# A row LSTM behind a group normalisation: first block's loads spread over the statistics, first chunk in four pieces, weights behind the fourth chunk, last block stored in two parts

## The chip, the cores and the metric

The kernel runs on one core of a Trainium2 chip. The metric is the device time in microseconds (us) of one execution. Six executions of the kernel before lie between 2173.32 and 2176.66 us. Engine names: PE is TensorE (matmul), PEld its weight loads, DVE is VectorE, ACT is ScalarE, POOL is GpSimd, SP is SyncE, which issues most DMAs.

## The reference, cut to what matters

```python
# x: (8, 96, 128, 128) float32
x = x + conv_lstm(group_norm(x))        # 32 groups of 3 channels, over whole images

def conv_lstm(X):                        # rows of the image are the time steps
    its = conv(X, W_is * mask)           # input-to-state, 384 outputs
    for row in range(128):
        gates = conv(h, W_ss) + its[row]
        f, i, o, g = ...                 # three sigmoids, one tanh
        c = f * c + i * g
        h = o * tanh(c)                  # h is the output row
```

The statistics need all of x (50.33 MB) before the first row can be normalised. Then 128 rows follow one another. Images are treated in two halves (s = 0, 1) of four, so there are 256 half steps, and the rows come in blocks of four (R = 4).

## The kernel before

Three parts matter: what the queues load before the recurrence, in which order VectorE works there, and the last store.

```python
# weights, issued from ScalarE at the start
nc.scalar.dma_start(wt[0:C, 0, :], w_ss[:, 0])
# ... six more weight loads, two of the bias, one of the group matrix, from ScalarE
nc.vector.tensor_add(wr[:, 0, :], wt[:, 0, :], wt[:, 3, :])
# ... three more sums on VectorE, one of the bias

def load_rows(s, k):           # 64 channels, once into each half of the partitions
    nc.sync.dma_start(xr[s][0:C2, :, 1:], rows_of(s, k, 0, C2))
    nc.sync.dma_start(xr[s][C2:P, :, 0 : R * W], rows_of(s, k, 0, C2))

def load(s, k):                # 32 channels into partitions 96-127, 96 into 0-95
    t = x_pool.tile([P, BH, R, W], F32, tag=f"x{s}", name=f"x{s}_{k}")
    flat = t.rearrange("c b r w -> c b (r w)")
    nc.sync.dma_start(flat[C:P], rows_of(s, k, C2, C))
    nc.sync.dma_start(flat[0:C], rows_of(s, k, 0, C))
    xt[s, k] = t

# statistics: 48 chunks of 128 x 8 KB through a ring of four tiles
for b in range(B):
    # ...
    for k in range(QW // CH):
        xc = ring[n % len(ring)]
        n += 1
        nc.sync.dma_start(xc, xb[:, bass.ts(k, CH)])
        for j in range(CH // SN):
            nc.vector.bn_stats(bst[:, k * (CH // SN) + j, :], xc[:, bass.ts(j, SN)])
        if n == len(ring):
            for s in range(NH):          # the first block, behind the fourth chunk
                load_rows(s, 0)
                load(s, 0)
    nc.vector.bn_aggr(st[:, b, :], bst.rearrange("c n s -> c (n s)"))

# products that nobody reads: 112 over 128, 64 and 32 rows; ten more just before the recurrence
# ...
# at the end of each row (in HalfStep.output): the residual
nc.gpsimd.tensor_add(xo, xo, h)
# at the end of each block of four rows:
def store(s, k):
    nc.sync.dma_start(out[... 4 rows ...], xt.pop((s, k))[0:C]...)
```

Call a load **wide** if it fills all 128 partitions (the chunks), and **narrow** if it fills 32, 64 or 96 of them (the eight DMAs of the first block, 4.19 MB together, in rows of 2 KB).

Of the kernel before, what the change touches and what calls it, by code (L numbers as in the profile page):

```python
# [7 lines left out]
F32 = mybir.dt.float32  # L8
# [7 lines left out]
def strided(ap, offset, dims):  # L16

    return bass.AP(ap.tensor, ap.offset + offset, [ap.ap[0], *[list(d) for d in dims]])
# [3 lines left out]
def kernel(  # L22
# [28 lines left out]
    nc = tc.nc  # L51
    B, C, H, W = x.shape
    P = 128
    NH = 2
    BH = B // NH
    R = 4
    NB = H // R
    J = W // 2
    JP = J + 2
    C2 = 64  # L60
    HW = H * W
    QW = C * HW // P
    CH = R * BH * W
# [3 lines left out]
    const = ctx.enter_context(tc.tile_pool(name="const", bufs=1))  # L67
    x_pool = ctx.enter_context(tc.tile_pool(name="xblk", bufs=2))
    g_pool = ctx.enter_context(tc.tile_pool(name="gates", bufs=2))
    ps_pool = ctx.enter_context(  # L70
        tc.tile_pool(name="ps", bufs=2, space=bass.MemoryType.PSUM)
    )
    ps_st = ctx.enter_context(
        tc.tile_pool(name="ps_st", bufs=1, space=bass.MemoryType.PSUM)
    )




    wt = const.tile([P, 5, 4 * C], F32, name="wt")  # L80
    wr = const.tile([P, 2, 4 * C], F32, name="wr")
    nc.scalar.dma_start(wt[0:C, 0, :], w_ss[:, 0])
    nc.scalar.dma_start(wt[C:P, 0, :], w_is[C2:C, 0])
    nc.scalar.dma_start(wr[0:C, 1, :], w_ss[:, 1])
    nc.scalar.dma_start(wr[C:P, 1, :], w_is[C2:C, 1])
    nc.scalar.dma_start(wt[0:C, 3, :], w_ss[:, 2])
    nc.gpsimd.memset(wt[C:P, 3, :], 0.0)
    nc.scalar.dma_start(wt[0:C2, 4, :], w_is[0:C2, 0])
    nc.scalar.dma_start(wt[C2:P, 4, :], w_is[0:C2, 1])

    for a in range(3):
        for j in range(4):
            third = a if j == 3 else j
            cols = bass.ds(a * P + j * 32, 32)
            if third < 2:
                nc.gpsimd.memset(wr[C:P, 1, cols], 0.0)
            if third < 1:
                nc.gpsimd.memset(wt[C:P, 4, cols], 0.0)
    nc.vector.tensor_add(wr[:, 0, :], wt[:, 0, :], wt[:, 3, :])
    nc.vector.tensor_add(wt[:, 1, :], wr[:, 0, :], wr[:, 1, :])  # L100
    nc.vector.tensor_sub(wt[:, 2, :], wr[:, 0, :], wr[:, 1, :])
    nc.vector.tensor_scalar_mul(wt[:, 1:3, :], wt[:, 1:3, :], 0.5)

    bias = const.tile([P, 3], F32, name="bias")
    bias2 = const.tile([P, 3], F32, name="bias2")
    nc.scalar.dma_start(bias, b_ss)
    nc.scalar.dma_start(bias2, b_is)
    nc.vector.tensor_add(bias, bias, bias2)
    gm = const.tile([P, 3, P], F32, name="gm")
    nc.scalar.dma_start(gm, gmat)  # L110


    def pair(shape, name):
# [20 lines left out]
    xt = {}  # L134

    def rows_of(s, k, lo, hi):
        return x[s * BH : (s + 1) * BH, lo:hi, k * R : (k + 1) * R, :].rearrange(
            "b c r w -> c b (r w)"
        )

    def load_rows(s, k):
        nc.sync.dma_start(xr[s][0:C2, :, 1:], rows_of(s, k, 0, C2))
        nc.sync.dma_start(xr[s][C2:P, :, 0 : R * W], rows_of(s, k, 0, C2))

    def load(s, k):
# [5 lines that stand above are left out]
# [5 lines left out]
    ] + [xn[s][1].rearrange("p r t b j -> p (r t b j)") for s in range(NH)]  # L156
    st = const.tile([P, B, 2], F32, name="st")
    n = 0
    for b in range(B):
        bst = g_pool.tile([P, QW // SN, 6], F32, tag="bst", name=f"bst{b}")  # L160
        xb = x[b].rearrange("c h w -> (c h w)").rearrange("(p q) -> p q", p=P)
        for k in range(QW // CH):
            xc = ring[n % len(ring)]
            n += 1
            nc.sync.dma_start(xc, xb[:, bass.ts(k, CH)])
            for j in range(CH // SN):
                nc.vector.bn_stats(bst[:, k * (CH // SN) + j, :], xc[:, bass.ts(j, SN)])
            if n == len(ring):
                for s in range(NH):
                    load_rows(s, 0)  # L170
                    load(s, 0)
        nc.vector.bn_aggr(st[:, b, :], bst.rearrange("c n s -> c (n s)"))



    def spin(rows, count):
        banks = [
            ps_pool.tile([P, 512], F32, tag=f"ps{a}", name=f"spin{a}_{rows}_{i}")
            for i in range(2)
            for a in range(2)  # L180
        ]
        for i in range(count):
            for q in range(P // rows):
                at = bass.ds(q * rows, rows)
                nc.tensor.matmul(  # L185
                    banks[(q * rows // 32 + i % (rows // 32)) % 4][:, 0:256],
                    wt[at, 0, 0:P],
                    wt[at, 0, 0:256],
                    start=True,
                    stop=True,  # L190
                    skip_group_check=True,
                )


    mean = const.tile([P, 3, B], F32, name="mean")
# [46 lines left out]
    NT = NB * R  # L242
# [4 lines left out]
    def inputs(s, row):  # L247

        h = hx[s][row // R % 2][:, row % R]
        vs, vf = gt("vs", s, row, (P, HB)), gt("vf", s, row, (P, HB))  # L250
        vd = gt("vd", s, row, (P, 2, HB))
        shaped = "p (b j) -> p b j"
        e, o = h[:, 0, :, 0:J], h[:, 1, :, 1 : J + 1]
        nc.vector.tensor_add(vs.rearrange(shaped, b=BH), e, o)  # L254
        last = nc.vector.tensor_sub(vf.rearrange(shaped, b=BH), o, e)  # L255
        diff = nc.gpsimd.tensor_sub(  # L256
            vd.rearrange("p t (b j) -> p t b j", b=BH),
            strided(h[:, 0, 0, :], 1, [(BH * JP - 1, 2), (JP, BH), (1, J)]),
            strided(h[:, 0, 0, :], 0, [(BH * JP + 1, 2), (JP, BH), (1, J)]),
        )  # L260
        tc.add_manual_dep(
            diff.ins,
            last.ins.name,
            mybir.DependencyInfo(mybir.DependencyClass.Sync, mybir.DependencyReason.SCHED_ONLY),
            reason="GpSimd starts when VectorE is done with both SBUF reads",
        )
        return vs, vf, vd

    class HalfStep:
# [62 lines left out]
        def output(self):  # L332

            s, row = self.s, self.row
            nxt = hx[s][(row + 1) // R % 2][0:C, (row + 1) % R]
            h = strided(nxt[:, 0, 0, :], 0, [(BH * JP + 1, 2), (JP, BH), (1, J)])
            shaped = "p (t b j) -> p t b j"
            nc.vector.tensor_mul(  # L338
                h,
                self.ps[2][0:C].rearrange(shaped, t=2, b=BH),  # L340
                self.th.rearrange(shaped, t=2, b=BH),
            )
            self.moving = inputs(s, row + 1) if row + 1 < NT else None
            xo = xt[s, row // R][0:C, :, row % R, :].rearrange("p b (j t) -> p t b j", t=2)
            nc.gpsimd.tensor_add(xo, xo, h)  # L345

    def store(s, k):
        nc.sync.dma_start(
            out[s * BH : (s + 1) * BH, :, k * R : (k + 1) * R, :].rearrange(
                "b c r w -> c b (r w)"  # L350
            ),
            xt.pop((s, k))[0:C].rearrange("c b r w -> c b (r w)"),
        )

    OWN, SHARED = ((0, 1), (2,), (), (3,)), ((), (0, 1), (2, 3), ())
# [1 line left out]
    def prepare(s, row):  # L357

        k, r = row // R + 1, row % R
        if k < NB:  # L360
            for j in OWN[r]:
                normalise_own(nc.gpsimd, s, k, j, 0, R)
                border(nc.gpsimd, s, k, j, 0, R)
            for j in SHARED[r]:
                normalise_shared(nc.gpsimd, s, k, j, 0, R)

    def finish(s, row):
        prepare(s, row)
        k = row // R
        if row % R == R - 1:  # L370
            if k + 2 < NB:
                load_rows(s, k + 2)
            store(s, k)
            if k + 2 < NB:
                load(s, k + 2)

    E = mybir.EngineType
    for count in (12, 4):
        for rows in (P, 64, 32):
            spin(rows, count)  # L380
    with tc.manual_schedule(engines={E.PE, E.Activation, E.DVE, E.Pool}):
        pm = ps_st.tile([P, 3, B], F32, tag="pm", name="pm")
        pv = ps_st.tile([P, 2, B], F32, tag="pv", name="pv")
        for i in (2, 0, 1):
# [4 lines left out]
        nc.vector.tensor_add(dq, dq, st[:, :, 1])  # L389
        for i in range(2):  # L390
            nc.tensor.matmul(pv[:, i, :], gm[:, i, :], dq, start=True, stop=True)
        spin(P, 10)
        nc.vector.tensor_scalar(v, pv, 1.0 / GQ, GN_EPS, ALU.mult, ALU.add)
        nc.scalar.activation(t1, v, AF.Sqrt)
        nc.scalar.activation(table, t1[:, 0, 0:1], AF.Sigmoid)
# [30 lines left out]
        for row in range(NT):  # L426
            for s in range(NH):
# [18 lines left out]
                if prev:  # L446
                    prev.cell_tanh()
                    prev.output()
                    moving[prev.s] = prev.moving
                    finish(prev.s, prev.row)  # L450
# [62 lines left out]
```

## Time and profile before

| | kernel before |
|---|---|
| time, median of 6 runs | 2174.74 us (2173.32 to 2176.66) |
| span of the profiled run | 2171.9 us |
| first product of the recurrence | 163.75 us |
| recurrence, first to last product | 1998.0 us |
| last product to the end | 10.1 us |
| VectorE busy, idle up to its last statistic | 121.6 us, and 31.0 us of waits |
| clock of TensorE in the recurrence | 1.00 |

The profile is read in this way. The page's slices give the busy tenths of each engine in 40 equal parts of the span, and below them the granted clock, the busy share of the DMA engines and their rate. The waits name for each engine and line who ended its idle time: us in total, times, longest. The timeline gives start and duration of instructions, with the idle time before the first in square brackets.

### The profile page before, as it was taken

The page shows a single profiled execution, that of the slowest core. Times are in us where ns is not written, and L with a number is a line of the kernel's source. Part 1 is how long each engine was busy: PE and PEld are TensorE (multiplying, and loading weights), DVE is VectorE, ACT ScalarE, POOL GpSimd, SP SyncE. Part 2 cuts the span into 40 slices and gives each one's busy share as a digit, 9 for nine tenths or more (in the row PEclk, how much of TensorE's full clock was granted, in tenths as well). Part 3 has the DMA queues.
Part 4 walks back from the last instruction along what each step waited for, and adds up shares of the span by engine and source line. Part 5 has one row for each costly group of instructions (what it writes and reads, how often), then busy time and mean ns, then how long its engine had stood idle before and what let it go on. Part 6 is the DMA issues. An engine that isn't in the chain of part 4 may idle for free.

```text
span 2171.9 us, 24875 instructions
## 1 busy us (share of the span) xinstructions
PE 2030.3 (93%) x7934; PEld 1465.1 (67%) x7934; DVE 1588.7 (73%) x3299; ACT 1351.5 (62%) x2572; POOL 1028.0 (47%) x1311
## 2 busy tenths in 40 slices
PE   4019999999999999999999999999999999999998
PEld 3017777777777777777777777777777777777775
DVE  4987777777777777777777777777777777777776
ACT  0006666666666666666666666666666666666665
POOL 0006555555555455555544555555455555555542
PEclk8559999999999999999999999999999999999999
DMA  9991444333444443334444332344443334444411
GB/s 304 421 336 39 107 107 107 80 74 74 93 107 107 107 96 78 77 71 106 107 107 107 88 78 76 80 107 107 107 107 81 75 74 92 107 107 107 100 37 29
DMA packets 103297, 237.42 MB, mean 109 GB/s; under 512 B 6304, under 2 KB 6912, under 8 KB 97024
## 3 DMA queue, kind: packets, MB, share of 16 engines
q1 hardware_dynamic: 102144, 234.90, 42.7%
q8 instruction: 64, 1.05, 0.2%
q10 hardware_dynamic: 1024, 0.94, 0.2%
q14 instruction: 65, 0.53, 0.1%
HBM read 185.49 MB, written 50.33 MB: 109 GB/s over the span
## 4 chain that ended last, share of the span: by engine, by line
PE 92%; DVE 0%; issue 0%; POOLq 0%; POOL 0%; ACT 0%
PE ps L283 92%; DVE hx L208 0%; POOLq L508 0%; POOL x L345 0%; DVE ps L300 0%; DVE ps L299 0%; DVE xn L208 0%; DVE hx L338 0%; DVE c L324 0%; ACT m L293 0%; DVE vs L254 0%; DVE nmr L402 0%; DVE rstd L401 0%; DVE nmr L403 0%; DVE t L399 0%
## 5 line engine op out<-in xcount | busy, mean ns | idle before, releaser
L283 PEld LDWEIGHTS ps<-vd,wt 128*128 128x128 f32 x3072 | 583.7, 190 | 407.1 <-issue 366.7
L283 PE MATMUL ps<-xn,wt 128*128 128x512 f32 x1536 | 795.3, 599 | 0.1
L283 PE MATMUL ps<-vd,wt 128*128 128x256 f32 x3072 | 788.4, 379 | 0.0
L256 POOL TENSOR_TENSOR vd<-hx 128x512 f32<-128x512 f32 x256 | 266.5, 1041 | 1080.2 <-DVE vf L255 895.0
L309 ACT ACTIVATE g<-ps 32x512 f32<-32x512 f32 x768 | 454.2, 591 | 468.6 <-PE ps L283 468.6
L293 ACT ACTIVATE m<-ps,bias 128x256 f32<-128x256 f32 x768 | 358.8, 467 | 169.6 <-PE ps L283 169.6
L283 PE MATMUL ps<-vs,wt 128*128 128x256 f32 x1536 | 456.9, 379 | 0.4 <-DVE vs L254 0.4
L283 PE MATMUL ps<-vf,wt 128*128 128x256 f32 x1536 | 456.8, 379 | 0.0
L317 DVE TENSOR_TENSOR ps<-ps,c 96x512 f32<-96x512 f32 x256 | 178.0, 695 | 376.8 <-ACT ps L313 376.8
L313 ACT ACTIVATE ps<-ps 96x512 f32<-96x512 f32 x768 | 442.9, 577 | 16.1
L300 DVE TENSOR_TENSOR ps<-m,ps 128x256 f32<-128x256 f32 x768 | 329.5, 429 | 26.3
L345 POOL TENSOR_TENSOR x<-x,hx 96x512 f32<-96x512 f32 x256 | 331.5, 1295 | 9.5 <-DVE hx L338 9.5
L299 DVE TENSOR_TENSOR ps<-m,ps 128x256 f32<-128x256 f32 x768 | 324.3, 422 | 15.9
L283 PEld LDWEIGHTS ps<-xn,wt 128*128 128x128 f32 x1536 | 270.7, 189 | 73.3 <-DVE ps L300 31.8
L283 PEld LDWEIGHTS ps<-vs,wt 128*128 128x128 f32 x1536 | 291.8, 190 | 40.4 <-PE spin L185 0.8
L283 PEld LDWEIGHTS ps<-vf,wt 128*128 128x128 f32 x1536 | 291.8, 190 | 39.7
L320 DVE TENSOR_TENSOR g<-ps,g 96x512 f32<-96x512 f32 x256 | 175.8, 687 | 107.1 <-ACT g L309 107.1
L208 POOL TENSOR_SCALAR hx<-x,rstd,nmr 32x512 f32<-32x512 f32 (+1 forms) x256 | 207.9, 812 | 25.4
L208 POOL TENSOR_SCALAR xn<-xr,rstd,nmr 128x512 f32<-128x512 f32 (+1 forms) x256 | 208.3, 814 | 0.2
L338 DVE TENSOR_TENSOR hx<-ps,th 96x512 f32<-96x512 f32 x256 | 173.9, 679 | 0.7 <-ACT th L328 0.7
L324 DVE TENSOR_TENSOR c<-ps,g 96x512 f32<-96x512 f32 x256 | 173.9, 679 | 0.0
L328 ACT ACTIVATE th<-c 96x512 f32<-96x512 f32 x256 | 157.9, 617 | 0.9 <-DVE c L324 0.9
(50 smaller groups left out, 443.3 us busy)
## 6 DMA issues: line engine op xcount, KB each, us to landing
xr<-in_x_dram SPq DMA_DIRECT2D x128, 512.0 KB, 9.3
x<-in_x_dram SPq DMA_DIRECT2D x64, 768.0 KB, 9.5
out_dram<-x SPq DMA_DIRECT2D x64, 768.0 KB, 5.4
xs<-in_x_dram SPq DMA_DIRECT2D x24, 1024.0 KB, 7.0
xn<-in_x_dram SPq DMA_DIRECT2D x24, 1024.0 KB, 6.9
x<-in_x_dram SPq DMA_DIRECT2D x64, 256.0 KB, 6.3
wt<-in_w_ss_dram ACTq DMA_DIRECT2D x2, 144.0 KB, 6.9
wt<-in_w_is_dram ACTq DMA_DIRECT2D x2, 96.0 KB, 6.6
```

The lines of the kernel that those rows point to most:

```text
L208: engine.tensor_scalar(dst, src, scale, shift, ALU.mult, ALU.add)
L256: diff = nc.gpsimd.tensor_sub(vd.rearrange("p t (b j) -> p t b j", b=BH), strided(h[:, 0, 0, :], 1, [(BH * JP - 1, 2), (JP, BH), (1, J)]), ...
L283: nc.tensor.matmul(o, wt[:, p, bass.ts(a, P)], rhs, start=start, stop=stop, skip_group_check=True)
L293: nc.scalar.activation(self.m1, self.ps[a][:, 0:HB], AF.Identity, bias=bias[:, a : a + 1])
L299: nc.vector.tensor_add(lo, self.m1, hi)
L300: nc.vector.tensor_sub(hi, self.m1, hi)
L309: nc.scalar.activation(self.g[a * 32 : (a + 1) * 32], self.ps[a][C:P], AF.Tanh)
L313: nc.scalar.activation(gate, gate, AF.Sigmoid)
L317: nc.vector.tensor_mul(f, f, cs[self.s].rearrange("p t b j -> p (t b j)"))
L320: nc.vector.tensor_mul(self.g, self.ps[1][0:C], self.g)
L324: nc.vector.tensor_add(c, self.ps[0][0:C], self.g)
L345: nc.gpsimd.tensor_add(xo, xo, h)
```

## The change

Its intent, as far as the code shows it: VectorE should start with the first quarter of the first chunk and not with the weights; the first block's loads should no longer stop the statistics in one lump; and the end should wait for a smaller store. The diff, cut to its core:

```diff
-    nc.scalar.dma_start(wt[0:C, 0, :], w_ss[:, 0])
+    def load_weights():
+        nc.sync.dma_start(wt[0:C, 0, :], w_ss[:, 0])
 ...                                    (all ten, now on SyncE)
+    def make_weights():                (memsets and VectorE's sums, called after the statistics)
 ...
+    first = [f for s in range(NH) for f in (lambda s=s: load_rows(s, 0), lambda s=s: load(s, 0))]
 ...
-            nc.sync.dma_start(xc, xb[:, bass.ts(k, CH)])
+            for piece in range(4 if n == 1 else 1):
+                size = CH // 4 if n == 1 else CH
+                nc.sync.dma_start(
+                    xc[:, bass.ts(piece, size)], xb[:, bass.ds(k * CH + piece * size, size)]
+                )
 ...
             if n == len(ring):
-                for s in range(NH):
-                    load_rows(s, 0)
-                    load(s, 0)
+                load_weights()
+            if n % 6 == 0 and first:
+                first.pop(0)()
 ...
-    (112 products over 128, 64 and 32 rows)
+    (96 products over 64 rows, chained through empty instructions of ScalarE)
 ...
-            nc.gpsimd.tensor_add(xo, xo, h)
+            (nc.gpsimd if row + 1 < NT else nc.vector).tensor_add(xo, xo, h)
 ...
-            store(s, k)
+            store(s, k, R - 1 if k + 1 == NB else 0, R)
 ...
+        elif k + 1 == NB and row % R == R - 2:
+            store(s, k, 0, R - 1)
```

More of the change, by code (lines that the diff above doesn't have):

```diff
@@ L69 @@
     g_pool = ctx.enter_context(tc.tile_pool(name="gates", bufs=2))
-    ps_pool = ctx.enter_context(
-        tc.tile_pool(name="ps", bufs=2, space=bass.MemoryType.PSUM)
-    )
-    ps_st = ctx.enter_context(
-        tc.tile_pool(name="ps_st", bufs=1, space=bass.MemoryType.PSUM)
-    )
     wt = const.tile([P, 5, 4 * C], F32, name="wt")
     wr = const.tile([P, 2, 4 * C], F32, name="wr")
-    nc.scalar.dma_start(wt[0:C, 0, :], w_ss[:, 0])
-    nc.scalar.dma_start(wt[C:P, 0, :], w_is[C2:C, 0])
@@ L84 @@
-    nc.scalar.dma_start(wr[0:C, 1, :], w_ss[:, 1])
-    nc.scalar.dma_start(wr[C:P, 1, :], w_is[C2:C, 1])
-    nc.scalar.dma_start(wt[0:C, 3, :], w_ss[:, 2])
-    nc.gpsimd.memset(wt[C:P, 3, :], 0.0)
-    nc.scalar.dma_start(wt[0:C2, 4, :], w_is[0:C2, 0])
-    nc.scalar.dma_start(wt[C2:P, 4, :], w_is[0:C2, 1])
-    for a in range(3):
-        for j in range(4):
-            third = a if j == 3 else j
-            cols = bass.ds(a * P + j * 32, 32)
-            if third < 2:
-                nc.gpsimd.memset(wr[C:P, 1, cols], 0.0)
-            if third < 1:
-                nc.gpsimd.memset(wt[C:P, 4, cols], 0.0)
@@ L99 @@
-    nc.vector.tensor_add(wr[:, 0, :], wt[:, 0, :], wt[:, 3, :])
-    nc.vector.tensor_add(wt[:, 1, :], wr[:, 0, :], wr[:, 1, :])
-    nc.vector.tensor_sub(wt[:, 2, :], wr[:, 0, :], wr[:, 1, :])
-    nc.vector.tensor_scalar_mul(wt[:, 1:3, :], wt[:, 1:3, :], 0.5)
     bias = const.tile([P, 3], F32, name="bias")
     bias2 = const.tile([P, 3], F32, name="bias2")
-    nc.scalar.dma_start(bias, b_ss)
-    nc.scalar.dma_start(bias2, b_is)
-    nc.vector.tensor_add(bias, bias, bias2)
     gm = const.tile([P, 3, P], F32, name="gm")
-    nc.scalar.dma_start(gm, gmat)
+    def load_weights():
+        nc.sync.dma_start(wt[0:C, 0, :], w_ss[:, 0])
+        nc.sync.dma_start(wt[C:P, 0, :], w_is[C2:C, 0])
+        nc.sync.dma_start(wr[0:C, 1, :], w_ss[:, 1])
+        nc.sync.dma_start(wr[C:P, 1, :], w_is[C2:C, 1])
+        nc.sync.dma_start(wt[0:C, 3, :], w_ss[:, 2])
+        nc.sync.dma_start(wt[0:C2, 4, :], w_is[0:C2, 0])
+        nc.sync.dma_start(wt[C2:P, 4, :], w_is[0:C2, 1])
+        nc.sync.dma_start(bias, b_ss)
+        nc.sync.dma_start(bias2, b_is)
+        nc.sync.dma_start(gm, gmat)
@@ new lines, in make_weights @@
+    def make_weights():
+        nc.gpsimd.memset(wt[C:P, 3, :], 0.0)
+        for a in range(3):
+            for j in range(4):
+                third = a if j == 3 else j
+                cols = bass.ds(a * P + j * 32, 32)
+                if third < 2:
+                    nc.gpsimd.memset(wr[C:P, 1, cols], 0.0)
+                if third < 1:
+                    nc.gpsimd.memset(wt[C:P, 4, cols], 0.0)
+        nc.vector.tensor_add(wr[:, 0, :], wt[:, 0, :], wt[:, 3, :])
+        nc.vector.tensor_add(wt[:, 1, :], wr[:, 0, :], wr[:, 1, :])
+        nc.vector.tensor_sub(wt[:, 2, :], wr[:, 0, :], wr[:, 1, :])
+        nc.vector.tensor_scalar_mul(wt[:, 1:3, :], wt[:, 1:3, :], 0.5)
+        nc.vector.tensor_add(bias, bias, bias2)
@@ L168 @@
             if n == len(ring):
-                for s in range(NH):
-                    load_rows(s, 0)
-                    load(s, 0)
+                load_weights()
+            if n % 6 == 0 and first:
+                first.pop(0)()
         nc.vector.bn_aggr(st[:, b, :], bst.rearrange("c n s -> c (n s)"))
-    def spin(rows, count):
-        banks = [
-            ps_pool.tile([P, 512], F32, tag=f"ps{a}", name=f"spin{a}_{rows}_{i}")
-            for i in range(2)
-            for a in range(2)
-        ]
-        for i in range(count):
-            for q in range(P // rows):
-                at = bass.ds(q * rows, rows)
-                nc.tensor.matmul(
-                    banks[(q * rows // 32 + i % (rows // 32)) % 4][:, 0:256],
-                    wt[at, 0, 0:P],
-                    wt[at, 0, 0:256],
-                    start=True,
-                    stop=True,
-                    skip_group_check=True,
-                )
+    make_weights()
@@ new lines, with follow @@
+    E = mybir.EngineType
+    ctx.enter_context(tc.manual_schedule(engines={E.PE, E.Activation}))
+    def follow(ins, other):
+        tc.add_manual_dep(
+            ins.ins,
+            other.ins.name,
+            mybir.DependencyInfo(mybir.DependencyClass.Sync, mybir.DependencyReason.DATA),
+            reason="TensorE's row tiles share a bank",
+        )
+    with tc.tile_pool(name="idle", bufs=1, space=bass.MemoryType.PSUM) as idle:
+        banks = [idle.tile([P, 512], F32, tag=f"i{n}", name=f"idle{n}") for n in range(6)]
+        relay = {}
+        for lag in (5, 1, 2, 3):
+            for k in range(12):
+                for q in range(2):
+                    n = (k - lag * q) % 6
+                    at = bass.ds(64 * q, 64)
+                    mm = nc.tensor.matmul(
+                        banks[n][:, 0:256],
+                        wt[at, 0, 0:P],
+                        wt[at, 0, 0:256],
+                        start=q == 0 or k < lag,
+                        stop=True,
+                        skip_group_check=True,
+                    )
+                    if n in relay:
+                        follow(mm, relay.pop(n))
+                    relay[n] = nc.scalar.nop()
+                    follow(relay[n], mm)
@@ new lines, with spin @@
+    ps_pool = ctx.enter_context(
+        tc.tile_pool(name="ps", bufs=2, space=bass.MemoryType.PSUM)
+    )
+    ps_st = ctx.enter_context(
+        tc.tile_pool(name="ps_st", bufs=1, space=bass.MemoryType.PSUM)
+    )
+    def spin(count):
+        bank = ps_pool.tile([P, 512], F32, tag="ps0", name="spin")
+        for i in range(count):
+            nc.tensor.matmul(
+                bank[:, 0:256],
+                wt[:, 0, 0:P],
+                wt[:, 0, 0:256],
+                start=True,
+                stop=True,
+                skip_group_check=True,
+            )
@@ L344, in output, with store @@
             xo = xt[s, row // R][0:C, :, row % R, :].rearrange("p b (j t) -> p t b j", t=2)
-            nc.gpsimd.tensor_add(xo, xo, h)
-    def store(s, k):
+            (nc.gpsimd if row + 1 < NT else nc.vector).tensor_add(xo, xo, h)
+    def store(s, k, lo, hi):
         nc.sync.dma_start(
-            out[s * BH : (s + 1) * BH, :, k * R : (k + 1) * R, :].rearrange(
+            out[s * BH : (s + 1) * BH, :, k * R + lo : k * R + hi, :].rearrange(
                 "b c r w -> c b (r w)"
             ),
-            xt.pop((s, k))[0:C].rearrange("c b r w -> c b (r w)"),
+            xt[s, k][0:C, :, lo:hi, :].rearrange("c b r w -> c b (r w)"),
         )
@@ L372, in finish @@
                 load_rows(s, k + 2)
-            store(s, k)
+            store(s, k, R - 1 if k + 1 == NB else 0, R)
             if k + 2 < NB:
                 load(s, k + 2)
-    E = mybir.EngineType
-    for count in (12, 4):
-        for rows in (P, 64, 32):
-            spin(rows, count)
-    with tc.manual_schedule(engines={E.PE, E.Activation, E.DVE, E.Pool}):
+        elif k + 1 == NB and row % R == R - 2:
+            store(s, k, 0, R - 1)
+    with tc.manual_schedule(engines={E.DVE, E.Pool}):
         pm = ps_st.tile([P, 3, B], F32, tag="pm", name="pm")
@@ L391 @@
             nc.tensor.matmul(pv[:, i, :], gm[:, i, :], dq, start=True, stop=True)
-        spin(P, 10)
+        spin(10)
         nc.vector.tensor_scalar(v, pv, 1.0 / GQ, GN_EPS, ALU.mult, ALU.add)
```

## The prediction

> **What bounds the kernel now.** I read the core's span and clock first, then the page's slices, the chain that ended last, stretches of the trace with the DMA share, the waits, and the timeline of both ends. The page's slices, the clock row and the rate row:
>
> ```profile
> PE   4019999999999999999999999999999999999998
> ...
> DVE  4987777777777777777777777777777777777776
> ...
> PEclk8559999999999999999999999999999999999999
> DMA  9991444333444443334444332344443334444411
> GB/s 304 421 336 39 107 107 107 80 74 74 93 107 107 107 96 78 77 71 106 107 107 107 88 78 76 80 107 107 107 107 81 75 74 92 107 107 107 100 37 29
> ```
>
> A slice is 54 us. Three of them are the group statistics (DMA and DVE full, PE not needed), 37 are the recurrence (PE full at full clock). The chain in order of time says the same in one piece:
>
> ```profile
> 163.75 2.83 PE ps L283 x12
> 166.57 0.07 issue
> 166.64 1988.21 PE ps L283 x7642
> ```
>
> So the run is 163.75 us before the first product, 1998 us of TensorE without a gap, and about 10 us of tail after the last product (2161.8 to 2171.9). The change leaves the 1998 us alone: the same 256 half steps, the same products. It works on the 163.75 and the 10.[...]
>
> What bounds the front is the question. Its waits, VectorE's and then the queue's own:
>
> ```profile
> DVE bst L167 <- DMA xs<-in_x_dram: 18.7, 1, 18.7
> DVE wr L99 <- DMA wt<-in_w_is_dram: 11.2, 1, 11.2
> ...
> SPq L165 <- DVE bst L167: 86.1, 41, 2.8
> ```
>
> VectorE starts at 11.24 us, since the weight sums stand first in its stream and wait for the weights; it eats four chunks, then idles 18.7 us until the fifth chunk. It looks as if 30 us of VectorE idle time were there to be won. The stretches with the DMA share say otherwise (columns: stretch and its length, busy us of PE, PEld, DVE, ACT, POOL with counts, clock, DMA share, GB/s):
>
> ```profile
> 2.00:11.00 9.00, 3.65 (x10) 3.04 (x11) 0.00 (x0) 0.21 (x1) 1.66 (x13) 1.00 0.92 304
> 11.00:18.00 7.00, 7.00 (x52) 5.96 (x52) 6.76 (x14) 1.07 (x1) 0.74 (x12) 1.00 0.95 349
> 18.00:38.00 20.00, 13.12 (x168) 10.99 (x164) 4.78 (x9) 0.00 (x0) 0.00 (x0) 0.91 1.07 222
> 38.00:150.00 112.00, 0.00 (x0) 0.00 (x0) 107.63 (x179) 0.00 (x0) 0.00 (x0) 0.50 1.01 413
> ```
>
> The DMA engines are full in every row. While VectorE idled (18 to 38 us) they carried the first block, 4.19 MB in rows of 2 KB, at only 222 GB/s; before and after they carried chunks at up to 422. From 38 us on VectorE and DMA are level: six chunks take VectorE 24 x 0.593 + 0.8 = 15.0 us (eight statistics take 4.83 us, so they start 0.593 apart), and 6.29 MB at 420 GB/s are also 15.0 us. So **DMA bounds the front**, and VectorE's late start was hidden beneath it.
>
> [...]xr is loaded in two halves, x in 32 and 96 partitions, at 222 GB/s. [...]the trace has 413 to 422 for whole chunks[...]. [...]304 and 349 GB/s in the first two rows, where both issue, are less than the 420 with one. [...]The trace: half until 161.4, 4.3 us after the ten warming products began at 157.07, and full when the recurrence starts at 163.75.
>
> **The change part by part.**
>
> 1. First block spread (one of four 1 MB loads after chunks 6, 12, 18, 24). It removes no byte and widens no load. Each load takes 1.05 MB / 222 GB/s = 4.7 us of all DMA engines, and VectorE, level with DMA, has no lead to bridge it. I expect four stalls of 3 to 5 us in place of one of 18.7, and no gain of its own, at most some 0.5 us at the seams.
>
> 2. First chunk in four pieces, statistics ahead of the weights. VectorE starts some 3.5 to 4 us into the span and not at 11.7. The first packets came at 2.0 us and a chunk takes 2.5, so chunk four is in at some 12.3 and VectorE is done with it at about 15. By itself this wins nothing, since chunk five comes later.
>
> 3. Weights behind the ring, ten issues on SP. Before, chunks three and four were issued only at 10.85 us (SP had waited 9.2 us for a weight load), and four chunks and the weights (4.19 + 0.94 MB, 10.0 + 3 us of DMA) were done at 18.4 instead of the possible 2.0 + 13 = 15: 3.4 us lost. Now the chunks go out at once. The ten issues (0.4 to 0.7 us each) partly wait for earlier loads to land, so chunk five is issued at about 15 and its packets begin at about 16.1 (issue to first packet was 0.75 to 2.0). **Gain 18.4 - 16.1 = 2.3 us.** After it there are the same 44 chunks (112 us with their disturbances) and 19 us of first block: the last chunk lands at 148.2 instead of 150.5.
>
> 4. Weight sums (0.56 + 0.54 + 0.55 + 0.55 + 0.16 = 2.3 us on VectorE) come after the statistics in program order. In one of the stalls they are free; behind the last statistics they cost up to 2. I give the latter one chance in four: **+0.5 us**.
>
> 5. Unread products. 112 warming products go (224 instructions, two for each product), 96 on 64-row tiles come, chained over ACT. They need wt alone, and even at 1 us a link they end near 16 + 96 = 112 us, before PE is wanted at about 151. The ten warming products before the recurrence stay. **0 us.**
>
> 6. Tail. The last add goes from POOL (1.29 us) to VectorE, where a product of that size takes 0.69: 0.6 us less. The last store shrinks from 4 rows to 1. The rows:
>
> ```profile
> 2164.53 0.69 DVE L338 TENSOR_TENSOR hx<-ps,th 96x512 f32<-96x512 f32 x1 [0.70 <-ACT th L328]
> 2165.30 1.29 POOL L345 TENSOR_TENSOR x<-x,hx 96x512 f32<-96x512 f32 x1 [4.87 <-DVE hx L338]
> 2166.61 0.32 SPq L348 DMA_DIRECT2D out_dram<-x  x1
> ```
>
> Of the 5.3 us from issue to the end, the packets of 2 KB took some 3 (2168 to 2171.1 in the trace's packet records, 24 on each of 16 engines). With 512 bytes each I estimate 1.1: 1.9 us less. **Together 2.5 us.**
>
> Sum: -2.3 + 0.5 - 2.5 = -4.3, so 2175.15 - 4.3 = 2170.9, about 2171 us.
>
> **The rivals.**
>
> A. *The stall was real.* If the spread loads slip in beside the chunks[...], VectorE bounds: 4 + 122 us of statistics and aggregation + some 3 us, an end near 129 to 135 instead of 153.8, and a time near 2152. For it: the stall stands in the waits with 18.7 us. Against it: DMA is full in all those stretches[...]. A partial overlap, a third of the 19 us, would give 2164 to 2165, and that is my lower end.
>
> B. *A new wait eats the gain.* Ten weight issues on the queue that carries the chunks, each waiting for a landing, could delay chunk five to 19 us or later, and the weight sums could come last. Then the front is no shorter or 2 us longer, and only the tail is won: 2172 to 2175.
>
> C. *TensorE changes.* The unread products before the recurrence are different, and if the pace of the 7680 products hung on what ran before, 0.2% would be 4 us. For it: only that somebody took pains over them. Against it: PE shows no gap, a full clock from 161.4 to its end, and both versions warm up with the same ten products.
>
> D. *The tail is hidden or fixed.* If the landing of the last store is mostly fixed cost, the tail gives 1 us instead of 2.5: 2172.5.
>
> **Range and chances.** Front 0 to -9 (B to a third of A), tail -1 to -3: 2164 to 2175 us should hold eight times in ten, most likely 2171. Faster by over 2% needs 43 us, more than all idle time of VectorE in the front: 0.01. Slower by over 2% would need C at a size for which nothing speaks: 0.01. Within 2%: 0.98.
>
> **What would show it.** Right: DMA share near 1 from 2 us to the last chunk; VectorE with four stalls of 3 to 5 us and a first statistic before 5 us; the narrow loads still near 220 GB/s; the first recurrence product 1 to 3 us earlier than 163.75; the recurrence 1998 us; the end 1.5 to 3 us nearer to the last product. Wrong: a front shorter by 8 us or more with VectorE unbroken (A); chunk five later than 21 us or weight sums after the last statistic (B); a recurrence that differs by over 2 us (C).

The sum came to -4.3 us. Three things in it are less than measurements. That the narrow loads could run no faster than 222 GB/s was the assumption; without it, the case against rival A rests on the DMA share alone. The 1.1 us for packets of 512 bytes is an estimate without a source (the trace of the changed kernel has 1.1 us). And 1 us a link for the unread products is an assumed upper end (measured: 96 products in 35.4 us).

## The result, and the profile after

| | before | after |
|---|---|---|
| time, median of 6 runs | 2174.74 us | 2179.35 us (2175.63 to 2183.4) |
| span of the profiled run | 2171.9 | 2177.9 |
| VectorE's first statistic | 11.72 | 3.58 |
| last aggregation of statistics begins | 153.01 | 161.73 |
| first product of the recurrence | 163.75 | 172.36 |
| recurrence | 1998.0 | 1998.1 |
| last product to the end | 10.1 | 7.4 |

The ratio is 1.0022, with a 95% interval of 1.0009 to 1.0035: slower, by some 0.2%. The runs also scatter more than before, over 7.8 us against 3.3.

So the span grew by 6.0 us: 8.6 more in front, 2.7 less at the end, and the recurrence stayed. First the waits of VectorE up to the recurrence, which before had one entry of 18.7 us, one time, and one of 1.1:

```profile
DVE bst L170 <- DMA xs<-in_x_dram: 19.4, 9, 4.2
DVE bst L170 <- DMA xn<-in_x_dram: 16.5, 9, 4.1
```

VectorE now waits 18 times, 35.9 us in all. It started 8 us earlier and lost more than it had won. The stretches show what DMA did meanwhile (length, busy us of PE, PEld, DVE, ACT, POOL, then the clock, the DMA share and GB/s):

```profile
60.00:80.00 20.00, 0.00 (x0) 0.00 (x0) 13.76 (x23) 0.00 (x0) 0.00 (x0) 0.50 1.03 333
80.00:100.00 20.00, 0.00 (x0) 0.00 (x0) 12.85 (x22) 0.00 (x0) 0.00 (x0) 0.50 1.03 332
...
140.00:145.00 5.00, 0.00 (x0) 0.00 (x0) 5.00 (x9) 0.00 (x0) 0.00 (x0) 0.50 1.01 413
```

DMA was full again by its share (1.01 to 1.03), which adds up the time that packets take and so counts a slowed packet as busy: it reads 1.03 at 333 GB/s and 1.01 at 413. But where a load of the first block falls it moved 332 GB/s over 20 us. By an estimate from the rates of the kernel before, wide chunks at 420 GB/s and 1.05 MB at 222 GB/s would have given (20 - 4.7) us x 420 + 4.7 us x 222 = 7.5 MB, or 373 GB/s. Some 2 us are missing in each of these stretches. One such load in the timeline of VectorE and the queue:

```profile
81.80 4.98 DVE L170 BATCH_NORM_STATS2 bst<-xs 128x6 f32<-128x512 f32 x8
82.19 0.42 SPq L146 DMA_DIRECT2D x<-in_x_dram  x1
82.67 0.42 SPq L147 DMA_DIRECT2D x<-in_x_dram  x1
84.30 2.85 SPq L166 DMA_DIRECT2D xs<-in_x_dram  x2
86.87 2.47 DVE L170 BATCH_NORM_STATS2 bst<-xn 128x6 f32<-128x512 f32 x4
...
92.13 2.47 DVE L170 BATCH_NORM_STATS2 bst<-xn 128x6 f32<-128x512 f32 x4 [2.79 <-DMA xn<-in_x_dram]
94.63 0.81 DVE L175 BATCH_NORM_AGGREGATE st<-bst 128x2 f32<-128x144 f32 x1
99.62 4.96 DVE L170 BATCH_NORM_STATS2 bst<-xs 128x6 f32<-128x512 f32 x8 [4.18 <-DMA xs<-in_x_dram]
```

The chunk that VectorE takes at 92.13 was issued ahead of the narrow load, and is 2.79 us late all the same; the chunk behind the load is 4.18 us late. I had expected only the second. The times at which the eight aggregations begin (one for six chunks) put a number on it. Before they are 15.0 to 15.1 us apart from the first to the seventh. After the change the four distances in which a load falls are 23.20, 21.60, 22.56 and 20.18: 27.4 us more than four times 15.03, where the burst takes some 19.6 us (its packets span 19.60 us in e1_burst below; in the kernel before all but the first and last 2% of them lie between 17.8 and 36.7 us).

At the end of the run the rows that answer to those of before:

```profile
2173.23 0.69 DVE L375 TENSOR_TENSOR hx<-ps,th 96x512 f32<-96x512 f32 x1 [0.69 <-ACT th L365]
2173.95 0.69 DVE L382 TENSOR_TENSOR x<-x,hx 96x512 f32<-96x512 f32 x1
```

The add takes 0.69 us on VectorE, and in the packet records the last store is 384 packets of 512 bytes between 2175.5 and 2176.6, 1.1 us where it was 3.2 (2 KB packets, 2167.4 to 2170.7).

### The profile page after: what moved, and what is told of

Its sections match the earlier page's. It is cut to its first block, busy times and chain, and to the rows that moved or that the text cites. A ratio compares the mean times of both kernels' runs of the same rounds, so it can differ in the third digit from the quotient of the medians.

```text
span 2177.9 us, 24915 instructions
## 1 busy us (share of the span) xinstructions
PE 2039.5 (94%) x7902; PEld 1466.4 (67%) x7902; DVE 1593.3 (73%) x3301; ACT 1350.3 (62%) x2572; POOL 1022.3 (47%) x1309
## 3 DMA queue, kind: packets, MB, share of 16 engines
q8 instruction: 64, 1.05, 0.2%
## 4 chain that ended last, share of the span: by engine, by line
PE 92%; DVE 0%; ACT 0%; issue 0%
PE ps L320 92%; DVE hx L245 0%; DVE xn L245 0%; DVE c L361 0%; DVE hx L375 0%; DVE g L357 0%; DVE x L382 0%; ACT th L365 0%; ACT g L346 0%; DVE vs L291 0%; DVE t L433 0%; DVE nmr L438 0%; DVE nmr L437 0%; DVE rstd L436 0%; DVE t L434 0%
```

## The experiments

My theory after reading the two traces: **DMA bounds the statistics, and each switch of the one queue between wide and narrow loads costs it something**, some 2 us for a group of narrow loads among chunks. Such a place, where chunks and narrow loads meet in the queue, is called a seam below. The burst pays that once, the changed kernel four times. Rivals: the front is longer because the weights now stand in the queue of the chunks; or because of the four pieces; or any foreign load among the chunks costs that; or the unread products matter after all. All twelve kernels gave correct results; each was timed in five rounds (runs counted: 4 or 5 of each).

| kernel | us | ratio to before (95%) | first product at |
|---|---|---|---|
| e1_burst | 2173.35 | 0.9998 (0.9984 to 1.0012) | 165.29 |
| e2_before_spread | 2182.70 | 1.0035 (1.0022 to 1.0048) | 173.10 |
| e3_before_tail | 2172.82 | 0.9994 (0.9981 to 1.0006) | 165.71 |
| e4_no_idle | 2179.61 | 1.0025 (1.0013 to 1.0038) | 171.63 |
| e5_eight | 2187.09 | 1.0061 (1.0048 to 1.0075) | 178.48 |
| e6_wide | 2184.72 | 1.0046 (1.0034 to 1.0059) | 177.40 |
| e7_narrow | 2199.78 | 1.0114 (1.0100 to 1.0128) | 192.52 |
| e8_row0 | 2155.45 | 0.9913 (0.9899 to 0.9926) | 148.34 |
| e9_act_queue | 2177.53 | 1.0013 (1.0001 to 1.0026) | 169.94 |
| e10_two_queues | 2171.25 | 0.9982 (0.9969 to 0.9994) | 164.34 |
| e11_whole | 2171.75 | 0.9984 (0.9970 to 0.9997) | 164.77 |
| e12_all_after | 2151.60 | 0.9897 (0.9879 to 0.9915) | 143.88 |

e9 to e11 ran on another chip than the rest; there the kernel before took 2175.21 us (2174.1 to 2176.09), and on the first 2174.16 to 2174.52 in three batches. Between batches I therefore compare ratios. In the batch of e1 to e4 the changed kernel did not run, but e4_no_idle, which differs from it by the unread products alone, did: 2179.61.

### e1_burst: the changed kernel, its loads in one burst again

```diff
             if n == len(ring):
                 load_weights()
-            if n % 6 == 0 and first:
-                first.pop(0)()
+                for load_first in first:
+                    load_first()
```

> The changed kernel with one part undone: the first block's four loads go out together behind the weights, as in the kernel before, and not after chunks 6, 12, 18, 24. Theory (seams: [...]worth 7.7 us by the aggregation times of the two traces): the front gets 7 to 8 us shorter, the first product of the recurrence near 164.5 instead of 172.35, time 2171 to 2172. Rival (the front is longer because of the weights on SP, the four pieces, or slower chunks on that chip): time stays at 2177 to 2180.

Measured: 2173.35 us, 6.0 less than the changed kernel. VectorE's waits have one long entry again:

```profile
DVE bst L170 <- DMA xs<-in_x_dram: 29.7, 5, 21.1
DVE bst L170 <- DMA xn<-in_x_dram: 2.0, 2, 1.1
```

The single wait of 21.1 us looks far worse than the waits of at most 4.2 in the changed kernel, and the front is 7.1 us shorter (165.29 against 172.36). The weights on SyncE, the pieces and the new products are all still in this kernel: they aren't what made it slower. Against e4, in the same batch, it is 6.3 us less. The gain was 6.0 and not the 7.7 that I had read from the traces; the profiled run of the changed kernel had also a stretch of slower chunks between 102 and 128 us (375 GB/s).

### e2_before_spread: the kernel before, with the spreading alone

```diff
-            if n == len(ring):
-                for s in range(NH):
-                    load_rows(s, 0)
-                    load(s, 0)
+            if n % 6 == 0 and first:
+                first.pop(0)()
```

> The kernel before with one part added: its first block's loads spread after chunks 6, 12, 18, 24. Theory (seams): 7 to 8 us slower than before, about 2182, VectorE with stalls on both sides of each load. My prediction's view (the bytes alone count): 2174 to 2175. Rival A of the prediction (overlap): 2165 or less.

Measured: 2182.70, 8.2 us slower than before (2174.52), as the theory had it. Here, too, the long wait for a chunk is gone from VectorE (the 11.4 us for the weights stay) and the front is 9 us longer:

```profile
DVE bst L168 <- DMA xn<-in_x_dram: 17.2, 7, 4.9
DVE bst L168 <- DMA xs<-in_x_dram: 8.6, 4, 3.0
```

So the spreading is both needed (e1) and enough (e2) for the loss.

### e3_before_tail: the kernel before, with the tail alone

```diff
-            nc.gpsimd.tensor_add(xo, xo, h)
+            (nc.gpsimd if row + 1 < NT else nc.vector).tensor_add(xo, xo, h)
 ... and the store of the last block as 3 rows and 1 row, as in the change
```

> The kernel before with only the tail changed: last add on VectorE, last block stored as 3 rows and 1 row. By the traces of before and after the stretch from the last product to the end goes from 10.1 to 7.4 us: 2.7 us faster, about 2172. Rival D (mostly fixed cost of the landing): 1 us.

Measured: 2172.82, 1.7 us less by the medians; the interval of the ratio holds 1, so the runs alone don't prove it. The traces do: from the last product to the end it is 7.6 us here and 10.1 in the kernel before; all twelve kernels with the changed tail read 7.4 to 7.6, and e2, with the old one, 10.1.

### e4_no_idle: the changed kernel without the chained products

```diff
-    with tc.tile_pool(name="idle", bufs=1, space=bass.MemoryType.PSUM) as idle:
-        ... (96 products over 64 rows, chained over ScalarE)
```

> The changed kernel without the chained products on 64-row tiles and their ACT links. Theory: no part in the time; front, recurrence (1998.2 us) and tail as in the changed kernel, 2176 to 2183 as its runs scatter. Rival C: the recurrence or the start of the clock differs, by over 2 us in the stretch from the first to the last product.

Measured: 2179.61, ratio 1.0025 against 1.0022 for the changed kernel. From the first to the last product it is 1998.1 us; the others lie between 1997.7 and 1998.1. The unread products in the statistics do nothing for the time.

### e5_eight: the eight narrow DMAs one by one

```diff
-    first = [f for s in range(NH) for f in (lambda s=s: load_rows(s, 0), lambda s=s: load(s, 0))]
+    first = [lambda s=s, i=i: part(s, i) for s in range(NH) for i in range(4)]   # part: one DMA
 ...
-            if n % 6 == 0 and first:
+            if n >= 6 and n % 3 == 0 and first:
```

> The changed kernel with the first block's eight DMAs spread singly (after chunks 6, 9, 12 ... 27) and not in four pairs. One group cost 2173.35 (burst), four groups 2179.35: 2.0 us for each group more. Theory (a cost for each switch between wide and narrow loads): seven groups more than the burst, 14 us, so about 2187. Rival (the cost comes with breaking up the burst at all, or with the ring of four running dry once, not with the number of switches): 2179 to 2181.

Measured: 2187.09. One, four and eight groups take 2173.35, 2179.35 and 2187.09: 2.0 us for each group from one to four, 1.9 from four to eight. The bytes and the loads are the same in all three; what grows is the number of times that chunks and narrow loads meet. VectorE's waits become still shorter and more, 28 of at most 3.6 us:

```profile
DVE bst L184 <- DMA xs<-in_x_dram: 21.1, 16, 3.6
DVE bst L184 <- DMA xn<-in_x_dram: 20.7, 12, 3.6
```

### e6_wide and e7_narrow: four more loads that nobody needs, wide or narrow

```diff
 # e6_wide, on e1_burst
+            if n in (6, 12, 18, 24):
+                for piece in range(4):          # 128 partitions, rows of 2 KB
+                    nc.sync.dma_start(xn[n // 6 % 2][0]...[:, bass.ts(piece, CH // 4)],
+                        xb[:, bass.ds(k * CH + piece * (CH // 4), CH // 4)])
 # e7_narrow, on e1_burst
+            if n in (6, 12, 18, 24):
+                load_rows(n // 6 % 2, 0)        # 64 + 64 partitions, rows of 2 KB
```

> The burst kernel (2173.35) plus four loads of 1 MB that nobody needs, after chunks 6, 12, 18, 24, each over all 128 partitions in four DMAs with rows of 2 KB, into a tile that is written again later. If the cost of the spread loads is that of narrow loads among wide ones: only their bytes, 4 x 2.5 to 2.8 us, so 2183.5 to 2185. Rival (any foreign load, or any load with 2 KB rows, among the chunks costs 2 us extra): 2191 to 2193.

> The burst kernel (2173.35) plus four loads of 1 MB that nobody needs at the same places, but narrow: the first block's rows once more into the two halves of the partitions (two DMAs of 512 KB with rows of 2 KB each). Theory: [...]27 us, 2200 to 2202. Without a switching cost: 20 us, 2193. If narrow loads cost no more than wide ones: 2184.

The 27 us in the theory for e7 are four times 4.9 us for the bytes (1.05 MB at the 214 GB/s of such loads in e1_burst) and 2 us for the group.

Measured: 2184.72 and 2199.78, so 11.4 and 26.4 us over e1_burst, 2.8 and 6.6 us for each load of 1.05 MB. The first is what the theory said, the second 0.2 us below its range and 6.8 above the 2193 without a cost for switches. Bytes, places and row length are the same in both. (What also differs, and no run varied, is how far apart the rows lie in x: 48 KB from partition to partition in the wide loads, 64 KB in the narrow ones.) A wide load costs its bytes (1.05 MB at 420 GB/s are 2.5 us) and 0.3 more. A narrow one costs 5.0 us by the rate of such loads in the burst (the pairs over 64 partitions ran at 207 to 214 GB/s there) and 1.6 more. The extra is a matter of narrow loads among wide ones, not of any foreign load. VectorE's waits in e7 are these; the 22.1 is the burst, which e7 has as well:

```profile
DVE bst L170 <- DMA xs<-in_x_dram: 41.6, 9, 22.1
DVE bst L170 <- DMA xn<-in_x_dram: 14.5, 7, 3.8
```

The packet records of the traces say who pays. Each chunk is 128 packets of 8 KB, which take 0.313 us each when chunks follow chunks. I add up what the packets of 8 KB took beyond that, until the last chunk is in, and divide by the 16 engines:

| kernel | mean of a packet of 8 KB, us | excess, us | last aggregation |
|---|---|---|---|
| e1_burst | 0.319 | 2.2 | 154.43 |
| after | 0.338 | 9.5 | 161.73 |
| e5_eight | 0.350 | 13.8 | 167.68 |
| e6_wide | 0.320 | 2.8 | 166.73 |
| e7_narrow | 0.334 | 8.0 | 181.89 |

From e1_burst to the changed kernel the excess grows by 7.3 us, and the last aggregation comes 7.3 us later. (In e5 the excess accounts for 11.6 of 13.3 us more than in e1_burst.) So the engines weren't idle: the chunks' own packets took longer, 0.47 to 0.62 us on the mean for those that began where both kinds were in flight (28 to 30, 50 to 52, 70 to 72 and 92 to 94 us in the changed kernel). Nor did the queue run dry there, as a ring of four tiles might make one think: from 64 to 74 us the DMA share is 1.04, at only 248 GB/s. A chunk that was issued ahead of a narrow load is still on some engines when others have gone on to that load: from 65 to 69 us, 3.4, 2.0, 1.2 and 0.6 of the packets in flight were of chunks, on the mean of each microsecond, beside 13 to 16 narrow ones.

### e9_act_queue: the spread loads on a second queue

```diff
-    first = [... (lambda s=s: load_rows(s, 0), lambda s=s: load(s, 0))]
+    first = [... (lambda s=s: load_rows(s, 0, nc.scalar), lambda s=s: load(s, 0, nc.scalar))]
 ...                                    (and each waits for the last statistic of its chunk)
-    (the chained products)
```

> The changed kernel without the chained products (2179.61 in e4), with the four spread loads issued from ScalarE when VectorE is done with chunk 6, 12, 18, 24, and so on a second queue beside the chunks. [...]the intent of the change, some 2165 to 2171. [...]2173 as in the burst. If every meeting of narrow and wide packets costs, as at the switches: 2180 or more.

The first two numbers: the first was meant for narrow and wide packets that run beside each other without cost, the second for packets that do not overlap.

Measured: 2177.53, ratio 1.0013 against 1.0025 for e4_no_idle, which has the same loads on one queue: some 2 to 2.6 us better, with intervals that overlap and on another chip, and still slower than the burst. The narrow packets now took 0.108 us each (0.159 in e4) and the packets of 8 KB 0.348 (0.334), an excess of 13.1 us: the cost moved from the one kind to the other. None of my three numbers was hit; the result lies between the second and the third. Note that these loads also start three chunks later than in the changed kernel, as they wait for VectorE and not for the queue.

### e10_two_queues: the two halves of the burst at the same time

```diff
-        nc.sync.dma_start(xr[s][C2:P, :, 0 : R * W], rows_of(s, k, 0, C2))
+        return q.dma_start(xr[s][C2:P, :, 0 : R * W], rows_of(s, k, 0, C2))   # q = nc.scalar
 ...                (flat[C:P] likewise; ScalarE's loads wait for the first statistic of chunk
                     four; the chained products are left out)
```

> The burst kernel (2173.35, here without the chained products) with the upper half of each narrow load (partitions 64 to 127, and 96 to 127) issued from ScalarE and the lower half from SyncE, at the same time. [...] Rival[...]: the burst takes 10 to 13 us, 2164 to 2167.

The rival: both halves move at once at up to the rate of the chunks (4.19 MB at 420 GB/s are 10 us).

Measured: 2171.25, ratio 0.9982 against 0.9998 for e1_burst: 2.1 us by the medians, 3.5 by the ratios, on another chip and with intervals that overlap. The burst itself can be read from the packet records: it lies between 18.24 and 36.67 us, 18.4 us where e1_burst has 19.6 (19.29 to 38.89). That is 6% less, far from the rival's 10 to 13 us. But the records name the queue of each packet, and the two queues were together in only a part of it. First ScalarE's alone had narrow packets in flight, then SyncE's alone, and from 29.5 us both (348 and 356 packets until 34):

```profile
18.20:22.40 4.20, 0.00 (x0) 0.00 (x0) 2.27 (x5) 0.00 (x0) 0.28 (x4) 1.00 1.01 208
22.60:29.40 6.80, 0.00 (x0) 0.00 (x0) 0.16 (x1) 1.28 (x1) 0.00 (x0) 1.00 1.07 214
29.50:34.00 4.50, 0.00 (x0) 0.00 (x0) 0.00 (x0) 0.00 (x0) 0.00 (x0) 1.00 1.05 320
```

So where the two halves really ran at the same time, they moved 320 GB/s, half as much again as one. The experiment did not test what it set out to for the rest of the burst; why the queues took turns until 29.5 us is open, and so is what a burst with both in flight throughout would take.

### e11_whole: the burst kernel with its first chunk in one load

```diff
-            for piece in range(4 if n == 1 else 1):
-                size = CH // 4 if n == 1 else CH
+            for piece in range(1):
+                size = CH
```

> The burst kernel (2173.35) with its first chunk in one load again. My prediction wanted 2.3 us from the early chunks and the weights behind them; burst and tail alone (2172.82) show none. If the four pieces with 2 KB rows eat it (the first 1 MB took until 6.5 us where 2.0 + 2.5 = 4.5 was counted): 1.3 to 2 us faster, 2171.3 to 2172. If the first packets are slow whatever their size: 2173 to 2174.

Measured: 2171.75, ratio 0.9984 against 0.9998: 1.6 us by the medians, 3 by the ratios. The first aggregation comes at 46.62 us and not at 48.22. The four pieces, meant to let VectorE start early, cost more than they give, since VectorE waits for the fifth chunk anyway. The stretch from 16 to 20 us shows where, e1_burst first and then e11:

```profile
16.00:20.00 4.00, 2.89 (x10) 1.45 (x12) 3.65 (x7) 0.00 (x0) 0.79 (x12) 1.00 0.57 124
16.00:20.00 4.00, 3.56 (x12) 1.51 (x12) 2.54 (x6) 0.00 (x0) 0.28 (x4) 1.00 0.87 199
```

Here the DMA engines did run dry, 43% of these 4 us with the pieces and 13% without. In both kernels SyncE stood still at the issues of the weights, waiting for chunks to land (L86 to L88: 7.3 us in e1_burst, 6.5 in e11), and the next loads were issued behind them: the first narrow one at 17.68 and 15.41 us. The intervals of e1 and e11 overlap, and they ran on different chips; the traces' 1.6 us and the expectation agree, so I take the sign as likely and the size as open.

### e8_row0 and e12_all_after: taking the narrow bytes out of the statistics

If DMA bounds the statistics, bytes taken out of it count in full, and most of the first block isn't needed before the recurrence: the first products need row 0 of partitions 96 to 127 of x and of xr, GpSimd takes up rows 1 to 3 after that, and the residual (partitions 0 to 95) comes later still (in the kernel before row 0 is normalised from 160.49 us on, rows 1 to 3 from 167.02, and the first residual comes at 181.44).

```diff
 # e8_row0, on e3_before_tail
             if n == len(ring):
                 for s in range(NH):
-                    load_rows(s, 0)
-                    load(s, 0)
+                    load_rows(s, 0, 0, 1)       # row 0 alone
+                    load_shared(s, 0, 0, 1)     # partitions 96-127, row 0 alone
 ...                                             (behind the loop over the chunks)
+    for s in range(NH):
+        load_shared(s, 0, 1, R)
+        load_rows(s, 0, 1, R)
+    for s in range(NH):
+        load_own(s, 0)                          # partitions 0-95
 # e12_all_after, on e11_whole: row 0, too, is loaded behind the last chunk
```

> A version meant to beat both: the kernel before with the changed tail, and of the first block only row 0 of the tiles that the first products need (0.75 MB of 4.19) ahead of the chunks; the rest follows the last chunk, where GpSimd and the residual need it later. Theory (DMA bounds the statistics, so bytes taken out of it count in full): the narrow loads in the front shrink from 19.6 us to 3 to 5, 14 to 16 us gained over the 2172.8 of the kernel with the tail alone, 2157 to 2160. Rival (GpSimd then waits for the rest and delays the second row, or VectorE bounds the statistics anyway): 2165 or more.

> The kernel of e11 (whole first chunk, weights behind the ring, changed tail) with nothing of the first block among the chunks: row 0 of what the first products need is loaded right behind the last chunk, then the rest. With no narrow load in the statistics, VectorE bounds them, and now its start counts: 15.03 us for six chunks, eight times, behind a start at 5 us with some 5 us lost at the weights. The last aggregation then comes near 129 to 132 (137.5 in the version with row 0 ahead), row 0 lands within the 7 us that the statistics' small products take, and the time is 2147 to 2151. Rival (GpSimd waits for the later rows, or row 0 comes too late): 2153 or more.

Measured: e8 2155.45, which is 17.4 us less than e3 and 19 less than before, and 1.5 better than expected. Its waits on chunks are almost gone:

```profile
DVE bst L174 <- DMA xs<-in_x_dram: 2.7, 2, 1.6
DVE bst L174 <- DMA xn<-in_x_dram: 0.9, 1, 0.9
```

Only now does VectorE bound the statistics, and only now is its start worth something: e12, where it starts at 6.18 us and not at 12.19 behind the first weight sum, takes 2151.60, 0.6 us beyond the upper end of what I expected and 1.0% below the kernel before (ratio 0.9897). Its last aggregation begins at 132.64 us against 137.53 in e8; the first product comes 11.2 us after that, where it was 10.8 in e8, so row 0 behind the last chunk gives about 0.4 us back.

## Why the prediction was wrong, point by point

- **The bound.** "DMA bounds the front" held. e6 (4.2 MB more of wide loads, 11.4 us more) and e8 (3.4 MB of narrow loads out of it, 17.4 us less) show it, and the burst with its long wait is the faster form (e1).
- **The first block spread: this step failed.** It said "no gain of its own, at most some 0.5 us at the seams", and "VectorE ... has no lead to bridge it. I expect four stalls of 3 to 5 us in place of one of 18.7". I counted the bytes at their rate and took the seams for free or a small gain. In their place the runs showed a cost of 2 us for each group of narrow loads among chunks (e1, the changed kernel, e5), waits on both sides of a load, and 6.0 us in the changed kernel, 8.2 in e2. The mechanism by which a narrow load slows the chunks next to it was in none of my rivals; rival B named a new wait, but at the weights (it came too, see the next point). The sign named for the bound, a DMA share near 1, could not have told: it stayed near 1 while the rate fell. Rival A (the loads slip in beside the chunks) is the opposite of what happened.
- **First chunk in four pieces and weights behind.** VectorE's first statistic came at 3.58 us, as predicted. "Chunk four is in at some 12.3" was wrong: it was in at 15.1. The first MB alone took until 7.07 us, and whole until 6.18 in e12, where I had counted 4.5. The gain of 2.3 us for the weights didn't show in the change (e1 lies 0.5 us above e3). That is rival B in part: SyncE waited 6.7 us at the weights' issues, chunk five was issued at 16.62 us, where some 15 was counted, the DMA share from 16 to 18 us was 0.63, and VectorE got chunk five at 21.67, past the 21 us that the prediction had named as B's sign. With a whole first chunk e11 has a ratio of 0.9984 against 0.9994 for e3, about what I had counted, within intervals that overlap.
- **Weight sums.** They ran from 17.53 to 19.85 us, in VectorE's wait for the fifth chunk, and cost nothing.
- **Unread products.** Right: no effect (e4). They ran from 15.70 to 51.11 us.
- **The tail.** Predicted 2.5 us; the traces show 2.7 (10.1 to 7.4), the runs of e3 1.7 by the medians.
- **Readings that were off.** Times that the prediction took from packet and clock records lie 0.2 to 0.9 us late against the profile's own: narrow loads from 17.3 to 17.8 us and not from 18.4 (so of the 2.3 us at most 1.7 was there to be won), full clock at 160.57 and not 161.4. And 222 GB/s is the mean of the burst: in e1_burst the loads over 64 partitions ran at 207 to 213 GB/s, that over 32 at 197, those over 96 at 223 to 240.
- **The sum.** Predicted -2.3 + 0.5 - 2.5. From the kernels that differ by one part it is -1.7 for the tail, +0.5 for the start (e1 over e3, within noise) and +6.0 for the spreading: +4.8, and 4.6 was measured. What stays open: why a seam costs 2 us (the packets carry no engine in my records; e9 only shows that a second queue shifts it), and why the changed kernel's runs scatter over 7.8 us.

## What to carry to other kernels

A long wait is worth only what the thing waited for could have done sooner: here the DMA engines were full, so one wait of 19 to 21 us and many short ones were the same bytes, and the short ones were dearer. Read the rate beside the busy share: a slowed engine counts as busy (a share of 1.04 at 248 GB/s in the changed kernel). In a stage that DMA bounds as here, don't scatter loads over 32 to 96 partitions among wide ones (2.0 us for each group here); keep them together, or better, take out of the bound stage what is not needed there (17 us won here in e8, against 6 lost by spreading). An earlier start of an engine pays only once that engine is the bound (e12 against e8).

## What else the traces show

- With one core at work, whole chunks moved at 410 to 422 GB/s (kernel before, stretches of 20 us from 40 to 140 us).
- First packets were slow. In the kernel before, the first 14 packets of 8 KB, which began between 1.77 and 2.10 us, took 0.82 us each, those that began at 3.2 to 4.2 us 0.31. It may be one reason why the first chunk came later than I had counted.
- From the first of the ten products just before the recurrence to full clock it was 3.5 us in the kernel before (157.07 to 160.57) and 3.1 in the changed one (165.79 to 168.8). But in this profile the clock reads 1.00 where no change was recorded earlier. In e4 it reads so until its first record at 169.40 us, though PE took only 6 product instructions in the 2 us from 166 us, and 11 in those from 170: as in the kernel before at clock 0.50 (6 from 158 us) and at 1.00 (11 from 161). So the mean clock of 0.999 in e4, e9 and e10, against 0.97 to 0.98 in the others, is no difference of the chip's.
